# Three scatters in flight with a GpSimd memset between them, and k2's seven products in another order

## The chip, the cores and the metric

The kernel runs on one core of one Trainium2 chip. The metric is the device time of one launch, in microseconds (us). Runs that are shown as "time" are launches without a profile; the profiled execution is one more launch, recorded by the hardware profiler, and its time is given beside them.

## The reference

One graph-attention layer and one gated feed-forward block over 384 nodes with 1024 features, both with a residual. Cut to what matters:

```
xn   = layernorm(x)                                   # 384 x 1024
q,k,v    = xn@wq.T+bq, xn@wk.T+bk, xn@wv.T+bv
q2,k2,v2 = q@wiq.T+biq, k@wik.T+bik, v@wiv.T+biv       # 16 heads of 64
mask = full((384,384), -inf); mask[src,dst] = softplus(w)[type-1]   # 12288 edges,
                                                      # the last edge of a cell wins
mask[i,i] = softplus(w)[3] where it is still -inf
out  = softmax(q2 k2^T / 8 + mask) v2                 # per head
x    = x + out@wo.T + bo
h    = silu(xn2@w1.T*s1) * (xn2@w2.T*s2)              # xn2 = layernorm(x)
h    = gelu(h@h1.T*..); h = gelu(h@h2.T*..)
x    = x + h@w3.T*s3
```

Edges are sorted by dst. Edge e lies in column e // 128 and partition e % 128 of a 128 x 96 table, so there are 96 mask columns of 128 edges each.

## The kernel before, in words

**Stages.** Layer normalisation and transposes come first, then the projections q, q2, v, v2, k and k2, then attention in 24 units (8 pairs of heads times 3 row tiles), the output projection, and the feed-forward block. The order on SyncE, ScalarE, VectorE and TensorE is the order of the program text (`manual_schedule`); on GpSimd only what is wrapped in `keep_in_program_order` is held to it.

**The mask.** The mask is built in a table in HBM, `tab`, with one word for each of the 147456 cells and some spare cells behind them. First a transfer fills it with the values without edges. Then each of the 96 columns is written by one indirect DMA on GpSimd (L366, the *scatter*), which puts 128 words of `val` at the cells of `cell`. Two scatters that are in flight together must not write the same cell. So VectorE first compares every edge of column c with the later edges of the columns that can be in flight with it (L350, `targets`), and an edge that has a later twin there is sent to a spare cell. `DEEP = 3` columns are in flight at most. The function `flight` says how many there are at column c: three in the groups of 16 columns that are listed in `DENSE`, and two in group 3 (columns 48 to 63). A scatter waits for the landing of the one that is `flight(c)` before it. Columns are handled in chunks of eight (`chunk`: `targets`, then `scatter`, then the next load of keys), and the calls of `chunk` are spread over the projections q to v2. When all 96 have been issued, GpSimd waits for the last three to land, reads the table back into SBUF as `mask` (L575) and goes on to its weight loads (L101: two halves of wo, later the feed-forward weights).

**Memory of the mask stage.** The tiles of this stage (`jp`, `bare`, `key`, `cell`, `val` and others in the pool `edge`, the key rows in the pool `krow`) are given back before attention; the pool `attn` is laid over the same addresses and holds, among others, `s1`, `s2`, `s4` of k2, the exponentials `e` and the transposed probabilities `pTb`.

**Products with seven multiplications.** The projections q2, v, v2, k and k2 use a 2 x 2 block scheme with seven block products instead of eight. It needs sums of blocks of the input (a11, a12, a21, a22; the sums are s1 to s4) and of the weights (b11, b12, b21, b22), which are formed in place: b12 becomes b22-b12 ahead of the products, b11 becomes b11+b12, b12 becomes b22-b11, b21 becomes b21-b11. For k2 these are in `project_k2` (L633): each entry of its list is a weight block, an input block and the work that VectorE or ScalarE does on the product, and a product lies in one of two PSUM buffers (`ps_mm`, `bufs=2`). The first half of k2 runs in one piece (L746) after its sums of the input have begun at L744; the second half is issued in small shares between the attention slots (L770).

What the sums of the input depend on and where they stand before:

```
nc.vector.tensor_add(s1, a21, a22)                       # L744
minus(s2, s1, a11)                                       # L745, shown as L414
for step, _ in enumerate(project_k2(0, slice(0, 2), 0)): # L746
    if step == 2 * HK:
        minus(a21, a11, a21)                             # a21 becomes s3, in place
        minus(s4, a12, s2)
```

Of the kernel before, what the change touches and what calls it, by code (L numbers as in the profile page):

```python
# [9 lines left out]
FP = mybir.dt.float32  # L10
# [14 lines left out]
P = 128  # L25
# [3 lines left out]
NCOL = E // P  # L29
HN = N // 2  # L30
HK = KF // 2
DEEP = 3
DENSE = (0, 1, 2, 4, 5)
CHUNK = 8
CELLS = N * N
EPS = 1e-5
# [8 lines left out]
def gnn_ffn_kernel(ctx: ExitStack, tc: tile.TileContext, x, edges, etw, vecs, rows,  # L45
# [4 lines left out]
    nc = tc.nc  # L50
# [148 lines left out]
    with tc.tile_pool(name="edge", bufs=1) as ep, tc.tile_pool(name="krow", bufs=2) as krp, \  # L199
# [114 lines left out]
        cnt = ep.tile([P, NCOL], FP, name="cnt")  # L314
        cell = ep.tile([P, NCOL], I32, name="cell")
        val = ep.tile([P, NCOL], FP, name="val")

        def values():

            ty = ep.tile([P, NCOL], I32, name="ty")  # L320
            nc.vector.tensor_scalar(ty, ed[:, 2, :], 3.0, None, op0=ALU.add)
            ty3 = ep.tile([P, NCOL], I32, name="ty3")
            nc.vector.tensor_single_scalar(ty3, ty, 3, op=ALU.bitwise_and)
            for j in range(4):
                vj = ep.tile([P, NCOL], FP, tag="vj", name="vj")
                nc.vector.tensor_scalar(vj if j else val, ty3, float(j), w8[:, j:j + 1],
                                        op0=ALU.is_equal, op1=ALU.mult)
                if j:
                    nc.vector.tensor_add(val, val, vj)
# [7 lines left out]
                                                    ap=[[0, P], [P, n], [1, P]]))  # L337
            return kr.rearrange("p c j -> p (c j)")

        def flight(c):  # L340

            return DEEP if c // 16 in DENSE else DEEP - 1

        def targets(c0, krf):

            for j in range(CHUNK):
                c = c0 + j
                w = min(flight(c + DEEP - 1), NCOL - c) * P
                jk = krp.tile([P, DEEP * P], BF, tag="jk", name="jk")
                nc.vector.scalar_tensor_tensor(jk[:, :w], krf[:, j * P:j * P + w], key[:, c:c + 1],  # L350
                                               later[:, :w], op0=ALU.is_equal, op1=ALU.mult,
                                               accum_out=cnt[:, c:c + 1])
            s = slice(c0, c0 + CHUNK)
            lost = krp.tile([P, CHUNK], FP, tag="lost", name="lost")
            nc.vector.scalar_tensor_tensor(lost, cnt[:, s], 0.0, spare, op0=ALU.is_gt, op1=ALU.mult)
            nc.vector.tensor_tensor(cell[:, s], key[:, s], lost, op=ALU.max)

        sent = []

        def after(ins, earlier):  # L360
            tc.add_manual_dep(ins, earlier.name, mybir.DependencyInfo(
                mybir.DependencyClass.Sync, mybir.DependencyReason.DATA), reason="table")

        def scatter(c0):
            for c in range(c0, c0 + CHUNK):
                i = nc.gpsimd.indirect_dma_start(  # L366
                    out=tab, in_=val[:, c:c + 1], in_offset=None,
                    out_offset=bass.IndirectOffsetOnAxis(ap=cell[:, c:c + 1], axis=0)).ins
                for other in sent[max(c - flight(c) + 1, 0):]:
                    tc.declare_no_dep(i, other, reason="no cell in common")  # L370
                for other in sent[max(c - DEEP, 0):max(c - flight(c) + 1, 0)]:
                    after(i, other)
                sent.append(i)

        krs = []
        asked = iter(range(0, NCOL, CHUNK))
# [7 lines left out]
        def chunk(more=True):  # L384

            c0 = len(sent)
            targets(c0, krs.pop(0))
            if c0 == 0:
                values()
            scatter(c0)  # L390
            if more:
                ask()
# [20 lines left out]
        def minus(to, a, b):  # L413
            nc.vector.tensor_tensor(to, a, b, op=ALU.subtract)  # L414

        def quarters(src, n):

            return [src[:, k:k + HK, r:r + n] for r in (0, n) for k in (0, HK)]

        def row_sums(src, n, **place):  # L420

            sums = act.tile([P, 4, HK, n], FP, name="sums", **place)
            s1, s2, s3, s4 = (sums[:, i] for i in range(4))
            a11, a12, a21, a22 = quarters(src, n)
            minus(s3, a11, a21)
            nc.vector.tensor_add(s1, a21, a22)
            minus(s2, s1, a11)
            minus(s4, a12, s2)
            return s1, s2, s3, s4
# [12 lines left out]
        def paired(w, g):  # L442

            w = w.rearrange("p k (g h c) -> p k g h c", h=2, c=P)[:, :, g]
            return [w[:, k:k + HK, :, h] for k in (0, HK) for h in (0, 1)]

        def paired_third(w):
            b11, b12, b21, b22 = paired(w, slice(0, 2))
            minus(b12, b22, b12)
# [59 lines left out]
        with tc.tile_pool(name="ps_st", bufs=6, space=bass.MemoryType.PSUM) as ps_st:  # L509
# [23 lines left out]
            c11, c12, c21, c22 = (v2[:, t, c:c + FH] for t in (0, 1) for c in (0, FH))  # L533
# [7 lines left out]
            def block(x, w):  # L541
                return product_R([(x[:, k, :], w[:, k, :]) for k in range(HK)])
# [8 lines left out]
            s1, s2, s3, s4 = row_sums(vT, P, tag="t", bufs=2)  # L551
# [6 lines left out]
            m7 = block(s3, b12)  # L558
            minus(b12, b22, b11)
            m6 = block(s2, b11)  # L560
            m2 = block(a12, b21)
# [4 lines left out]
            m5 = block(s1, b12)  # L566
# [49 lines left out]
    with tc.tile_pool(name="attn", bufs=1) as ap, \  # L616
# [7 lines left out]
        s1, s2, s4 = (ap.tile([P, HK, HN], FP, name=f"s{i}") for i in (1, 2, 4))  # L624
        a11, a12, a21, a22 = quarters(kT, HN)
# [3 lines left out]
        def flush():  # L629
            while waiting:  # L630
                waiting.pop()()

        def project_k2(half, g, lag):  # L633


            b11, b12, b21, b22 = paired(wik[half], g)
            c = k2T[:, 4 * half:4 * half + 4, :].rearrange("p (g h) n -> p g h n", h=2)[:, g]
            c11, c12, c21, c22 = (c[:, :, h, r:r + HN] for r in (0, HN) for h in (0, 1))
            n = g.stop - g.start

            def copies(ps):
                nc.scalar.copy(c11, ps)
                nc.scalar.copy(c12, ps)
                nc.vector.tensor_add(b11, b11, b12)

            def finish(to, ps, more, h):
                for i in range(n):
                    o = BIK + 4 * half + 2 * (g.start + i) + h
                    nc.vector.scalar_tensor_tensor(to[:, i, :], ps[:, i, :], vec[:, o:o + 1],  # L649
                                                   more[:, i, :], op0=ALU.add, op1=ALU.add)  # L650

            def m2(ps):
                finish(c11, ps, c11, 0)
                minus(b21, b21, b11)

            def m7(ps):
                nc.vector.tensor_add(c22, ps, c12)
                minus(b12, b22, b11)

            def m5(ps):  # L660
                nc.vector.tensor_add(c12, ps, c12)
                finish(c22, ps, c22, 1)

            for w, x, use in ((b11, a11, copies), (b21, a12, m2),
                              (b11, s2, lambda ps: nc.vector.tensor_add(c12, ps, c12)),
                              (b12, a21, m7), (b21, a22, lambda ps: finish(c21, ps, c22, 0)),
                              (b12, s1, m5), (b22, s4, lambda ps: finish(c12, ps, c12, 1))):
                ps = ps_mm.tile([P, 2, 256], FP, tag="mm", name="ps")
                for i in range(n):
                    for k in range(HK):  # L670
                        nc.tensor.matmul(ps[:, i, :HN], lhsT=w[:, k, i, :], rhs=x[:, k, :],  # L671
                                         start=(i, k) == (0, 0), stop=(i, k) == (n - 1, HK - 1))
                        if i * HK + k == lag - 1:
                            flush()
                        yield
                waiting.append(lambda ps=ps[:, :n, :HN], use=use: use(ps))
                if lag == 0:
                    flush()
            if g.stop == 2:
                early.append(load_w(*ffn[half], rounded=True))  # L680
# [61 lines left out]
        loaded = small.tile([P, 1], FP, name="loaded")  # L742
        nc.scalar.activation(loaded, eps, AF.Exp)
        nc.vector.tensor_add(s1, a21, a22)  # L744
        minus(s2, s1, a11)  # L745
        for step, _ in enumerate(project_k2(0, slice(0, 2), 0)):  # L746
            if step == 2 * HK:
                minus(a21, a11, a21)
                minus(s4, a12, s2)
        paired_third(wik[1])  # L750
        k2 = chain(*(project_k2(1, slice(g, g + 1), 3) for g in range(2)))
        steps, done, pairs = 2 * 7 * HK, 0, 0
        for s, new in enumerate(slots):
# [8 lines left out]
            for i in range(2):  # L762
# [6 lines left out]
                if i == 0:  # L769
# [7 lines left out]
                    if s in (9, 10):  # L777

                        ps = ps_mm.tile([P, 512], FP, tag="mm", name="ps")
# [226 lines left out]
```

## Time and profile before

| what | value |
|---|---|
| time, median of 3 runs | 404.39 us (403.07 to 406.37) |
| profiled execution, its own time | 408.77 us |
| its span, first to last instruction | 406.7 us |
| TensorE busy | 385.8 us, 95% of the span |
| VectorE busy | 258.7 us, 64% |
| GpSimd busy | 126.4 us, of which 116.2 us are the 96 scatters |
| mean granted TensorE clock | 0.983 |

The span is shorter than the profiled execution's own time by 2.1 us, which lie around it. The profiled execution is 4.4 us longer than the median of the runs; a sum of durations from the profile is made against 408.77 us. In the profile a line of the timeline reads: start, duration, engine, source line, operation, output and inputs, count, and in brackets how long the engine sat idle before it and what ended that.

### The profile page before, as it was taken

The page shows a single profiled execution, that of the slowest core. Times are in us where ns is not written, and L with a number is a line of the kernel's source. Part 1 is how long each engine was busy: PE and PEld are TensorE (multiplying, and loading weights), DVE is VectorE, ACT ScalarE, POOL GpSimd, SP SyncE. Part 2 cuts the span into 40 slices and gives each one's busy share as a digit, 9 for nine tenths or more (in the row PEclk, how much of TensorE's full clock was granted, in tenths as well). Part 3 has the DMA queues.
Part 4 walks back from the last instruction along what each step waited for, and adds up shares of the span by engine and source line. Part 5 has one row for each costly group of instructions (what it writes and reads, how often), then busy time and mean ns, then how long its engine had stood idle before and what let it go on. Part 6 is the DMA issues. An engine that isn't in the chain of part 4 may idle for free.

```text
span 406.7 us, 5195 instructions
## 1 busy us (share of the span) xinstructions
PE 385.8 (95%) x1925; PEld 294.0 (72%) x1925; DVE 258.7 (64%) x664; ACT 103.4 (25%) x233; POOL 126.4 (31%) x116
## 2 busy tenths in 40 slices
PE   7899999999999999999689988899999999999993
PEld 7555589999997444899479955566555444699983
DVE  5695959985898777454237587878766115622455
ACT  4611110000000000200000056775555138332420
POOL 3033447786764488568730000000000000200000
PEclk9999999999999999999959999999999999999998
DMA  7799996357227500940057072220941400290004
GB/s 275 260 356 277 302 327 236 93 191 262 66 66 264 201 0 2 358 158 2 0 187 285 0 233 80 63 93 6 318 144 53 156 0 0 67 348 0 1 4 155
DMA packets 29227, 59.90 MB, mean 147 GB/s; under 512 B 5424, under 2 KB 8336, under 8 KB 29072
## 3 DMA queue, kind: packets, MB, share of 16 engines
q1 hardware_dynamic: 20976, 45.90, 32.9%
q0 software_dynamic: 7936, 13.23, 10.6%
q10 hardware_dynamic: 288, 0.41, 0.3%
q8 instruction: 17, 0.28, 0.3%
q14 instruction: 10, 0.08, 0.1%
HBM read 57.26 MB, written 2.26 MB: 146 GB/s over the span
## 4 chain that ended last, share of the span: by engine, by line
PE 86%; DVE 8%; ACT 2%; issue 2%; DMA 1%; SPq 0%; ACTq 0%
PE ps L457 28%; PE ps L601 10%; PE ps L151 10%; PE ps L538 9%; PE ps L671 7%; PE ps L870 6%; PE av L730 4%; PE ps L882 4%; PE pp L721 3%; PE sc L689 3%; DVE e L703 2%; DVE e L713 1%; DMA xs<-in_x 1%; DVE y L965 1%; DVE y L964 1%
## 5 line engine op out<-in xcount | busy, mean ns | idle before, releaser
L366 POOL DMA_INDIRECT tab<-val,cell x96 | 116.2, 1210 | 84.3 <-DMA tab<-val,cell 32.2
L350 DVE SCALAR_TENSOR_TENSOR jk<-kr,key,jp 128x384 bf16<-128x384 f32 (+1 forms) x96 | 50.3, 588 | 5.7 <-DMA kr<-keyd 5.7
L601 PE MATMUL ps<-wo,aT 128*128 128x512 f32 x96 | 43.0, 595 | 0.0
L151 PE MATMUL ps<-xT,wq 128*128 128x384 f32 x128 | 41.5, 487 | 0.3 <-ACT xT L266 0.3
L151 PEld LDWEIGHTS ps<-xT,wq 128*128 128x128 f32 x128 | 24.2, 190 | 17.2 <-ACT xT L266 0.5
L705 ACT ACTIVATE e<-e,lo 128x384 f32<-128x384 f32 x48 | 29.0, 605 | 27.5 <-DVE lo L703 27.4
L601 PEld LDWEIGHTS ps<-wo,aT 128*128 128x128 f32 x96 | 17.5, 190 | 19.4 <-issue 18.5
L870 PE MATMUL ps<-x,w 128*128 128x384 f32 (+2 forms) x176 | 25.8, 306 | 0.0
L457 PE MATMUL ps<-xT,wk 128*128 128x192 f32 x96 | 21.2, 374 | 4.7 <-issue 4.6
L101 POOL DMA_DIRECT2D w<-in_w x3 | 2.5, 847 | 74.1 <-PE ps L671 54.5
L870 PEld LDWEIGHTS ps<-x,w 128*128 128x128 f32 x176 | 25.1, 190 | 0.5 <-issue 0.5
L703 DVE CUSTOM_DVE_ANT_0 e<-sc,mask 128x384 f32<-128x384 f32 x48 | 23.9, 553 | 1.0 <-PE sc L689 1.0
L538 PE MATMUL ps<-wiv,vT 128*128 128x512 f32 x56 | 24.5, 592 | 0.0
L457 PEld LDWEIGHTS ps<-xT,wk 128*128 128x128 f32 x96 | 19.0, 222 | 7.1 <-issue 7.0
L721 PEld LDWEIGHTS pp<-ident,e 128*128 128x128 f32 x144 | 16.2, 141 | 10.9 <-issue 6.7
L671 PE MATMUL ps<-kT,wik 128*128 128x192 f32 x128 | 22.8, 328 | 1.1 <-DVE k2T L649 1.1
L671 PEld LDWEIGHTS ps<-kT,wik 128*128 128x128 f32 x128 | 20.7, 190 | 2.2 <-DVE k2T L649 2.0
L457 PE MATMUL ps<-sums,wk 128*128 128x192 f32 x128 | 21.5, 327 | 0.5 <-issue 0.5
L457 PEld LDWEIGHTS ps<-sums,wk 128*128 128x128 f32 x128 | 20.9, 190 | 0.9 <-issue 0.7
L721 PE MATMUL pp<-ident,e 128*128 128x128 f32 x144 | 20.6, 278 | 0.7 <-ACT pTb L766 0.5
L457 PE MATMUL ps<-sums,wiq 128*128 128x192 f32 x128 | 21.1, 326 | 0.0
L457 PE MATMUL ps<-sums,wv 128*128 128x192 f32 x128 | 21.1, 326 | 0.0
(168 smaller groups left out, 591.7 us busy)
## 6 DMA issues: line engine op xcount, KB each, us to landing
kr<-keyd SPq DMA_DIRECT2D x11, 640.0 KB
raw<-in_w SPq DMA_DIRECT2D x12, 512.0 KB
w<-in_w POOLq DMA_DIRECT2D x3, 2048.0 KB
wiq<-in_wiq SPq DMA_DIRECT2D x2, 2048.0 KB
wv<-in_wv SPq DMA_DIRECT2D x2, 2048.0 KB
wiv<-in_wiv SPq DMA_DIRECT2D x2, 2048.0 KB
wk<-in_wk SPq DMA_DIRECT2D x2, 2048.0 KB
wik<-in_wik SPq DMA_DIRECT2D x2, 2048.0 KB
```

The lines of the kernel that those rows point to most:

```text
L151: nc.tensor.matmul(ps[:, :N], lhsT=w[:, k, o * P:(o + 1) * P], rhs=src[:, k, :], start=(k == 0), stop=(k == nk - 1))
L350: nc.vector.scalar_tensor_tensor(jk[:, :w], krf[:, j * P:j * P + w], key[:, c:c + 1], later[:, :w], op0=ALU.is_equal, op1=ALU.mult, accum_ ...
L366: i = nc.gpsimd.indirect_dma_start(out=tab, in_=val[:, c:c + 1], in_offset=None, out_offset=bass.IndirectOffsetOnAxis(ap=cell[:, c:c + 1], ...
L457: nc.tensor.matmul(ps[o // 2][:, o % 2, :HN], lhsT=w[:, k, o * P:(o + 1) * P], rhs=x[:, k, :], start=(o % 2, k) == (0, 0), stop=(o % 2, k) ...
L538: nc.tensor.matmul(ps, lhsT=x, rhs=w, start=i == 0, stop=i == len(steps) - 1)
L601: nc.tensor.matmul(ps, lhsT=aT[:, k, t * P:(t + 1) * P], rhs=wos[half][:, k, :], start=k == start, stop=k == end - 1)
L671: nc.tensor.matmul(ps[:, i, :HN], lhsT=w[:, k, i, :], rhs=x[:, k, :], start=(i, k) == (0, 0), stop=(i, k) == (n - 1, HK - 1))
L703: nc.vector.tensor_tensor_reduce(e, sc[:, :N], mask[:, t, :], -0.125, 3e38, op0=ALU.add, op1=ALU.min, accum_out=lo)
L705: nc.scalar.activation(e, e, AF.Exp, bias=lo, scale=-1.0, accum_out=dens[u][:, j:j + 1])
L721: nc.tensor.transpose(pt[:, m, :], e[:, m * P:(m + 1) * P], ident)
L730: nc.tensor.matmul(av[j * D:(j + 1) * D, :N], lhsT=v2[:, m, h * D:(h + 1) * D], rhs=pTs[pair % 2][:, j * NT + m, :], start=(m == 0), stop= ...
L870: nc.tensor.matmul(ps[:, rows], lhsT=w[:, k, o * P:(o + 1) * P], rhs=x[:, k, rows], start=n == 0, stop=n == len(todo) - 1)
```

## The change

1. `DENSE` and `flight` go. Every column may have three scatters in flight, and every `targets` instruction compares over three columns (384 numbers wide, where 16 of them were 256 wide).
2. After each scatter GpSimd writes zeros into a new tile `pace` of 128 x 512 float32. Scatter and memset are both kept in program order, so that one memset lies between any two scatters, and one behind the last.
3. `project_k2` takes its seven products in another order. Product by product, as weight block times input block, before: b11 a11, b21 a12, b11' s2, b12 s3, b21' a22, b12' s1, b22 s4. After: b11 a11, b21 a12, b12 s3, b22 s4, b11' s2, b21' a22, b12' s1. A prime marks a weight block that has been replaced in place by a sum. The product b11' s2 is now added to two outputs (c12 and c22) by two instructions where one sufficed.
4. All four sums of the input (s1, a21 replaced by s3, s2, s4) are formed before the first product of k2's first half; two of them were formed during its second product.

```
-DENSE = (0, 1, 2, 4, 5)
+PACE = 512
...
+        pace = ep.tile([P, PACE], FP, name="pace")
...
-                w = min(flight(c + DEEP - 1), NCOL - c) * P
+                w = min(DEEP, NCOL - c) * P
...
-                i = nc.gpsimd.indirect_dma_start(
+                send = nc.gpsimd.indirect_dma_start(
                     out=tab, in_=val[:, c:c + 1], in_offset=None,
-                    out_offset=bass.IndirectOffsetOnAxis(ap=cell[:, c:c + 1], axis=0)).ins
-                for other in sent[max(c - flight(c) + 1, 0):]:
+                    out_offset=bass.IndirectOffsetOnAxis(ap=cell[:, c:c + 1], axis=0))
+                tc.keep_in_program_order(send)
+                i = send.ins
+                for other in sent[1 - DEEP:]:
                     tc.declare_no_dep(i, other, reason="no cell in common")
-                for other in sent[max(c - DEEP, 0):max(c - flight(c) + 1, 0)]:
-                    after(i, other)
+                if c >= DEEP:
+                    after(i, sent[-DEEP])
                 sent.append(i)
+                tc.keep_in_program_order(nc.gpsimd.memset(pace, 0.0))
...
+            def m6(ps):
+                nc.vector.tensor_add(c12, ps, c12)
+                nc.vector.tensor_add(c22, ps, c22)
...
-            for w, x, use in ((b11, a11, copies), (b21, a12, m2),
-                              (b11, s2, lambda ps: nc.vector.tensor_add(c12, ps, c12)),
-                              (b12, a21, m7), (b21, a22, lambda ps: finish(c21, ps, c22, 0)),
-                              (b12, s1, m5), (b22, s4, lambda ps: finish(c12, ps, c12, 1))):
+            for w, x, use in ((b11, a11, copies), (b21, a12, m2), (b12, a21, m7),
+                              (b22, s4, lambda ps: finish(c12, ps, c12, 1)), (b11, s2, m6),
+                              (b21, a22, lambda ps: finish(c21, ps, c22, 0)), (b12, s1, m5)):
...
         nc.vector.tensor_add(s1, a21, a22)
+        minus(a21, a11, a21)
         minus(s2, s1, a11)
-        for step, _ in enumerate(project_k2(0, slice(0, 2), 0)):
-            if step == 2 * HK:
-                minus(a21, a11, a21)
-                minus(s4, a12, s2)
+        minus(s4, a12, s2)
+        for _ in project_k2(0, slice(0, 2), 0):
+            pass
```

## The prediction

> **What bounds the kernel now.** I read the page first, then the waits of GpSimd, then the timeline around the place where mask and k2 meet, the table by stage for the clock, and last the waits of TensorE in the attention part.
>
> ```profile
> PE 385.8 (95%) x1925; PEld 294.0 (72%) x1925; DVE 258.7 (64%) x664; ACT 103.4 (25%) x233; POOL 126.4 (31%) x116
> PE 86%; DVE 8%; ACT 2%; issue 2%; DMA 1%; SPq 0%; ACTq 0%
> L366 POOL DMA_INDIRECT tab<-val,cell x96 | 116.2, 1210 | 84.3 <-DMA tab<-val,cell 32.2
> ```
>
> TensorE holds 86% of the chain that ended last, GpSimd none of it. But 96 scatters of 1.21 us, each with a gap of 0.30 us ahead of it, fill the time from 26.4 to 204.6 us, and this stream has little to spare:
>
> ```profile
> POOL tab L366 <- DMA tab<-val,cell: 32.2, 15, 4.7
> POOL tab L366 <- issue: 23.3, 75, 0.8
> POOL tab L366 <- DVE jk L350: 3.8, 3, 2.1
> ```
>
> Only some 38 us are real waiting, 32.2 us of it for landings. The rest is work and the gap. Where the stream ends:
>
> ```profile
> 188.85 2.28 DVE L414 TENSOR_TENSOR wk<-wk 128x2048 f32<-128x2048 f32 x1
> 189.72 2.25 POOL L366 DMA_INDIRECT tab<-val,cell  x1 [0.30 <-issue]
> 192.27 0.96 POOL L366 DMA_INDIRECT tab<-val,cell  x1 [0.31 <-issue]
> ...
> 202.39 0.96 POOL L366 DMA_INDIRECT tab<-val,cell  x1 [0.30 <-issue]
> 203.65 0.96 POOL L366 DMA_INDIRECT tab<-val,cell  x1 [0.30 <-issue]
> ...
> 206.42 0.80 POOL L575 DMA_DIRECT2D mask<-tab  x1 [1.81 <-DMA tab<-val,cell]
> ...
> 213.13 0.96 DVE L744 TENSOR_TENSOR s<-kT 128x768 f32<-128x768 f32 x1
> ...
> 230.45 0.92 PE L689 MATMUL sc<-k2T,q2T 64*128 64x384 f32 x4
> ...
> 232.35 0.55 DVE L703 CUSTOM_DVE_ANT_0 e<-sc,mask 128x384 f32<-128x384 f32 x1
> ```
>
> See three things. The last scatters run back to back, 1.265 us apart. The last one lands just ahead of 206.4 us, when the read of the mask starts. And L744, the first sum of k2's input, starts at 213.13 us. L744 writes into the memory that the mask stage gave back. The views leave semaphore instructions out, but the records of the trace hold four of them at L744, from 212.4 to 212.7 us, which name the eight counters on which the scatters land. So k2's sums wait for the last of the 96 scatters, not only for kT. Before, the scatters are 7 us early (206.4 against 213.1 us).
>
> The 7 us are a loan: kT itself is late, because TensorE stumbles while the last scatters run.
>
> ```profile
> 190.00:196.00 6.00, 6.00 (x38) 5.88 (x37) 1.69 (x2) 0.00 (x0) 4.85 (x4) 1.00 0.02 0
> 200.00:202.00 2.00, 0.78 (x4) 0.50 (x3) 0.00 (x0) 0.00 (x0) 1.70 (x2) 0.92 0.02 1
> 202.00:204.00 2.00, 0.99 (x4) 0.77 (x4) 0.00 (x0) 0.00 (x0) 1.39 (x3) 0.50 0.02 0
> 208.00:212.00 4.00, 4.00 (x15) 4.00 (x14) 0.84 (x3) 0.00 (x0) 0.17 (x1) 0.51 0.95 319
> ```
>
> (Columns: stretch, length, busy us and count of PE, PEld, DVE, ACT, POOL, then clock, DMA share, GB/s.) From 196.4 to 206.8 us only 16 matmuls run, where 16 x 0.163 us = 2.6 us would do; the next 17 take 5.5 instead of 2.8 us at half clock. That is 10.5 us lost, and it ends with the last landing. No wait is named; the scatters are the only other thing going on.
>
> **What the Trainium skill says.** *Perfetto Trace Analysis*, section "DMA Instruction — SWDGE (GPSIMD)": the recorded end of such a DMA is that of its descriptors, not of its data. The trace agrees: the last scatter ends at 204.6 us and its landing is still waited for until 206.4. *SBUF — State Buffer*, "Who interferes with whom": a VectorE instruction with two SBUF inputs holds up a GpSimd instruction that reads SBUF, not one that only writes. The trace agrees on the first half: the scatter at 189.72 us lasts 2.25 us, until the L414 of 188.85 us ends. A memset only writes. *TensorE: Matmul & The Clock Gate*, "What's actually happening": idleness of a few us halves the clock until it has been busy for a while. Here it stayed at 0.50 from about 202 to 212 us.
>
> **The change part by part.**
>
> *The memset.* Nearest rows, from the start of the profile:
>
> ```profile
> 0.74 0.20 POOL masks.py:197 MEMSET ident<- 128x128 f32 x1 [0.29 <-POOLq L998]
> 0.89 1.06 POOL L209 MEMSET mask<- 128x1152 f32 x1
> ```
>
> (1.06-0.20)/1024 = 0.84 ns per number, so 512 numbers last 0.20 + 384 x 0.00084 = 0.52 us. Starts of neighbours overlap by 0.05 us (0.74+0.20 against 0.89), which leaves 0.48 us of the queue for each, 46 us in all. Bounds: if the 0.30 us gap ahead of a scatter passes while the memset runs, only about 0.20 us each are added; if the memset pays such a gap of its own, 0.78. I take 0.48: when a scatter had waited for a landing it also began 0.27 us after it, so the gap looks like work of GpSimd itself, which a memset on the same engine can't hide; and the small memsets at the start follow each other within 0.03 us, so a memset has no such gap.
>
> *Where the scatters then end.* Columns 0 to 19 (26 to 72 us) are bound by landings, with 16 us of waits: memsets fall mostly into them. I give this stage 3 us more, 75 us. Then no wait is left to speak of, since three periods of 2 us cover the 2 to 6 us of a landing, and the two-in-flight waits of columns 51, 53 and 55 (7.8 us in all) go. The period is the scatter's mean in its stretch + 0.30 + 0.48. Means by stretch: 72 to 113 us 30.88/24 = 1.29; 113 to 143 16.26/14 = 1.16; 143 to 178 25.04/19 = 1.32; 178 to 206 20.73/20 = 1.04. So 24 columns at 2.07 reach 125 us; 9 at 1.94 reach 143; 17 at 2.10 reach 178; 13 at 1.82 reach 202; the last 12 at 0.96 + 0.78 = 1.74, with VectorE standing, start until 223, and the last lands 2 us later: **225 us** instead of 206.
>
> *What waits for it.* L744 on VectorE, and behind it in order the other sums, all of b11', b21', b12' and the evictions that free PSUM. TensorE can do products 1 and 2 (5.2 us) and stops at product 3, which needs s3. The mask read, wo and the feed-forward weights queue behind the scatters on GpSimd too, but mask was there some 20 us before L703 asked for it, and is again early: it is read at 225 us and asked for at about 245. L744 moves from 213.1 to 225.1 us: +12.0. Whether TensorE's stumble goes doesn't matter then; what it saves is waited away.
>
> *From L744 to L703.* Before 232.35 - 213.13 = 19.2 us. After: s1 and s3 take 2.0 us (0.96 + 0.95 and the hand-over); products 3 to 7 are 5 x 16 x 0.163 = 13.0, the first of them at half clock after the idle stretch, +2.6; then add 0.56, finish 0.74, L414 1.22: 20.1. So +0.9. The other two sums, b11' and b21' (0.95 + 0.95 + 1.22 + 0.74 + 1.22 us) fit beside products 3 and 4.
>
> *k2's second half.* Its stops of TensorE in the attention part:
>
> ```profile
> PE ps L671 <- DVE wik L644: 1.9, 1, 1.9
> PE ps L671 <- DVE wik L414: 1.7, 1, 1.7
> ```
>
> b11' and b12' now have two and one more products of slack, so these 3.6 us can go; against them stand two extra adds of 0.35 us on VectorE, which is the next in the chain there. Bounds -3.6 to +0.7; I take -2.
>
> *The rest.* 16 `targets` instructions are 128 numbers wider: about 0.13 us each on VectorE, which has 27 us free between 72 and 143 us. Nothing.
>
> Sum: +12.0 + 0.9 - 2 = +10.9 on 408.8, 419.7 us in the profile's own time. That time was 4.4 us over the median of the runs; the same offset gives **415 us** for the median.
>
> **The rivals.**
>
> *A, the stumble goes and the stream is in time (faster).* If the gap of 0.30 us passes under the memset, 76 columns gain 0.27 each: the end is about 225 - 20 = 205, landing 206. TensorE, no longer disturbed by back-to-back scatters, reaches k2 at 202 and product 3 at 207 instead of 217; L744 at 206 lets it start at 208. That is -9.5 and -2, with no cold clock: 397 us in the profile's time, 393 on the median; if the runs without a profile stumble less (they are 4.4 us shorter), about 400. I put it at 397. It decides once the scatters land before 210. For it: the stumble ends with the last landing. Against: the 0.27 us after a landing.
>
> *B, a draw.* Scatters land at 211 to 215: what the stumble gave is taken by the wait. About 404 us. It needs a memset of 0.3 us.
>
> *C, worse.* The memset pays its own gap partly: 0.64 each, landing at 237, +24 instead of +12: 427 us.
>
> *D, the memset does not space the scatters* (GpSimd works on both at once): then 7.8 us of waits go, landing near 198, the stumble stays and kT with it; -2 from the second half: 402 us.
>
> **How the numbers follow.** Forecast (landing 217 to 232) 0.58; C 0.09; A 0.19; B 0.09; D 0.05. The forecast's own range is 408 to 422 us. The 80% range takes C's edge and most of A: 396 to 427. A measurement of this kernel can tell about 1% from no change. Faster by over 1% (below 400.3): 0.21; within 1%: 0.12; slower (above 408.4): 0.67.
>
> **What would show it.** Right: starts of scatters 1.7 us apart where nothing else disturbs, L744 beginning within a us of the last landing, a hole in TensorE of over 8 us after k2's second product, half clock behind it; no stop at L644 or L414 later. Wrong: scatters still 1.3 us apart, or L744 later than the last landing by several us. The forecast falls if the last scatter starts before 210 us.

## The result, and the profile after

The changed kernel takes 423.19 us (median of 4 runs, 420.57 to 423.53) against 404.62 us before (median of 4 runs, one more than in the table of before): a ratio of 1.0443, 95% interval 1.0384 to 1.0503. It is slower by 4.4%. The profiled execution after took 423.14 us with a span of 421.3 us; against the profiled span before, 406.7 us, that is +14.6 us.

The page of the changed kernel, the lines that answer to those shown of before (busy time and share by engine; the chain; then line, engine, operation, count, busy us, mean ns, idle time before):

```profile
PE 383.2 (91%) x1925; PEld 293.7 (70%) x1925; DVE 261.4 (62%) x667; ACT 103.4 (25%) x233; POOL 180.8 (43%) x212
PE 47%; POOL 27%; DVE 9%; DMA 9%; issue 4%; ACT 2%; SPq 0%; POOLq 0%; ACTq 0%; DVEq 0%
L363 POOL DMA_INDIRECT tab<-val,cell x96 | 118.9, 1238 | 52.3 <-DVE val L330 22.0
L373 POOL MEMSET pace<- 128x512 f32 x96 | 51.9, 541 | 0.1
```

TensorE does the same work (383.2 us busy), but its part of the chain has fallen from 86% to 47%, and GpSimd, which held none of it, holds 27%: the scatters (L363) and the memsets (L373) have become the path that sets the end. The 51.9 us of memsets are new; what the scatters waited for landings fell from 32.2 to 16.6 us, as GpSimd's waits show (who waited for what: us in total, times, longest):

```profile
POOL tab L363 <- DMA tab<-val,cell: 16.6, 15, 2.8
POOL mask L575 <- DMA tab<-val,cell: 1.3, 1, 1.3
```

The timeline of the changed kernel where mask and k2 meet:

```profile
223.97 0.97 POOL L363 DMA_INDIRECT tab<-val,cell  x1 [0.17 <-issue]
224.94 0.54 POOL L373 MEMSET pace<- 128x512 f32 x1
225.64 0.96 POOL L363 DMA_INDIRECT tab<-val,cell  x1 [0.17 <-issue]
...
227.90 0.96 DVE L747 TENSOR_TENSOR s<-kT 128x768 f32<-128x768 f32 x1 [25.70 <-DMA tab<-val,cell]
228.40 0.79 POOL L575 DMA_DIRECT2D mask<-tab  x1 [1.26 <-DMA tab<-val,cell]
...
229.99 4.24 PE L674 MATMUL ps<-kT,wik 128*128 128x192 f32 x16 [23.38 <-DVE kT L414]
...
246.92 0.55 DVE L706 CUSTOM_DVE_ANT_0 e<-sc,mask 128x384 f32<-128x384 f32 x1
```

Read the brackets. The first sum of k2's input (L747, which was L744) stood still for 25.70 us, and a landing in `tab` released it. TensorE had done products 1 and 2 by 206.6 us and then waited 23.38 us for the block that replaces a21. The table by stage shows the hole and the half clock behind it (stretch, length, busy us and count of PE, PEld, DVE, ACT, POOL, clock, DMA share, GB/s):

```profile
206.00:212.00 6.00, 0.62 (x4) 0.32 (x2) 0.00 (x0) 0.00 (x0) 5.50 (x8) 0.75 0.01 0
212.00:220.00 8.00, 0.00 (x0) 0.00 (x0) 0.00 (x0) 0.00 (x0) 7.17 (x11) 0.50 0.01 0
230.00:238.00 8.00, 8.00 (x41) 8.00 (x42) 6.94 (x10) 0.00 (x0) 1.02 (x2) 0.82 1.00 356
```

From 212 to 220 us GpSimd is the only one of these engines that works. Before the hole, from 196 to 206 us, TensorE no longer stumbles: its last product of kT ends at 201.4 us in place of 212.3. Those 11 us are waited away.

### The profile page after: what moved, and what is told of

The parts are those of the page before. It is cut to its first block, busy times and chain, and to the rows that moved or that the text cites. A ratio compares the mean times of both kernels' runs of the same rounds, so it can differ in the third digit from the quotient of the medians.

```text
span 421.3 us, 5295 instructions
## 1 busy us (share of the span) xinstructions
PE 383.2 (91%) x1925; PEld 293.7 (70%) x1925; DVE 261.4 (62%) x667; ACT 103.4 (25%) x233; POOL 180.8 (43%) x212
## 4 chain that ended last, share of the span: by engine, by line
PE 47%; POOL 27%; DVE 9%; DMA 9%; issue 4%; ACT 2%; SPq 0%; POOLq 0%; ACTq 0%; DVEq 0%
POOL tab L363 19%; PE ps L601 10%; PE ps L151 10%; POOL pace L373 8%; DMA tab<-val,cell 8%; PE ps L873 6%; PE ps L674 6%; PE av L733 4%; PE ps L885 4%; PE pp L724 3%; PE sc L692 2%; DVE e L706 2%; PE ps L457 1%; DVE e L716 1%; DMA xs<-in_x 1%
## 5 line engine op out<-in xcount | busy, mean ns | idle before, releaser
L363 POOL DMA_INDIRECT tab<-val,cell x96 | 118.9, 1238 | 52.3 <-DVE val L330 22.0
L347 DVE SCALAR_TENSOR_TENSOR jk<-kr,key,jp 128x384 bf16<-128x384 f32 (+1 forms) x96 | 52.5, 611 | 4.4 <-DMA kr<-keyd 4.4
L373 POOL MEMSET pace<- 128x512 f32 x96 | 51.9, 541 | 0.1
L674 PE MATMUL ps<-kT,wik 128*128 128x192 f32 x128 | 25.6, 349 | 27.7 <-DVE kT L414 23.4
L674 PEld LDWEIGHTS ps<-kT,wik 128*128 128x128 f32 x128 | 22.4, 203 | 29.4 <-issue 23.6
L101 POOL DMA_DIRECT2D h<-in_h x2 | 1.5, 752 | 62.7 <-issue 62.7
L457 PEld LDWEIGHTS ps<-sums,wiq 128*128 128x128 f32 x128 | 20.9, 190 | 0.0
```

Of the source, the lines that this page charges most:

```text
L363: send = nc.gpsimd.indirect_dma_start(out=tab, in_=val[:, c:c + 1], in_offset=None, out_offset=bass.IndirectOffsetOnAxis(ap=cell[:, c:c + ...
L373: tc.keep_in_program_order(nc.gpsimd.memset(pace, 0.0))
L457: nc.tensor.matmul(ps[o // 2][:, o % 2, :HN], lhsT=w[:, k, o * P:(o + 1) * P], rhs=x[:, k, :], start=(o % 2, k) == (0, 0), stop=(o % 2, k) ...
```

## The experiments

The theory under test: the scatters' last landing gates k2's first sum, because attention's memory was the mask stage's, and the memset moves this landing. Rivals: the new order of k2's products costs the time; or the hole has another cause. Each kernel of this section was timed beside runs of the kernel before on its own chip; ratios are against those. "Landing" is the time at which the read of the mask starts. The read waits for the last landing and starts about 0.6 us behind it (in the changed kernel the last scatter started at 225.64 us and landed 2.13 us later, at 227.77), so a first sum that the landing releases stands some 0.5 us before the figure in this column. The times to the right of the ratio are those of one profiled execution each. In three of these (k2's order only, reused memory out of the way, before without its last 20 scatters) TensorE had also stood still for 1.6, 2.1 and 2.5 us near 77 us: VectorE, late after a late load of keys, was late with an eviction of q2. What follows there comes 2 to 3 us later for that reason alone.

| kernel | time, us | ratio, 95% interval | landing, us | k2's first sum, us | first exponential, us |
|---|---|---|---|---|---|
| before (profile shown above) | 404.62 | 1 | 206.4 | 213.1 | 232.3 |
| changed | 423.19 | 1.0443 (1.0384 to 1.0503) | 228.4 | 227.9 | 246.9 |
| no memset | 398.93 | 0.9871 (0.9792 to 0.9951) | 204.4 | 203.9 | 222.5 |
| k2's order only | 401.64 | 0.9935 (0.9906 to 0.9965) | 210.1 | 209.6 | 228.7 |
| scatter part only | 424.28 | 1.0497 (1.0411 to 1.0583) | 227.2 | 226.7 | 247.1 |
| changed, reused memory out of the way | 410.55 | 1.0153 (1.0072 to 1.0234) | 228.9 | 204.8 | 233.4 |
| memset of 64 | 401.57 | 0.9912 (0.9869 to 0.9954) | 208.5 | 208.0 | 226.6 |
| memset of 1024 | 452.9 (one run) | | 257.8 | 257.2 | 277.8 |
| no memset, memory out of the way | 399.81 | 0.9877 (0.9833 to 0.9921) | 206.0 | 207.0 | 225.7 |
| before, once more | 402.84 (one run) | | 206.7 | 207.5 | 225.9 |
| memory out of the way, tail paced | 398.20 | 0.9827 (0.9778 to 0.9877) | 214.0 | 202.5 | 222.2 |
| no memset, memory out of the way, again | 400.53 | 0.9880 (0.9824 to 0.9935) | 206.0 | 207.0 | 225.6 |
| before, without its last 20 scatters | 398.12 | 0.9823 (0.9775 to 0.9871) | 181.8 | 205.3 | 224.5 |

**One part away: no memset.**

```
-                tc.keep_in_program_order(nc.gpsimd.memset(pace, 0.0))
```

> The changed kernel without the memset: three scatters in flight throughout, k2's new order. Theory (the landing of the last scatter gates k2's first sum): scatters 1.27 us apart again, the two-in-flight waits gone, so the last landing is at 196 to 200 us in place of 227.7; the first sum starts when kT is done, 201 to 212 us, and the time is 394 to 404 us. Rival (the new order of the products costs the time): it stays at 418 to 424 us. Rival (the stumble of TensorE comes from back-to-back scatters): PE has a hole ahead of the last landing again, near 190 to 199 us, and half clock.

Measured: 398.93 us. The loss is gone and a gain is left. Three in flight and the fixed order on GpSimd are still in this kernel, so neither of them carries the loss. The last landing came at about 204 us, some 4 us later than expected, since 18 waits for landings still took 30.9 us: without the memset, three in flight fill up again. The group of k2's first sum in this kernel, its idle time last:

```profile
L745 DVE TENSOR_TENSOR s<-kT 128x768 f32<-128x768 f32 x1 | 1.0, 959 | 1.6 <-DMA tab<-val,cell 1.6
```

Even here the landing releases the sum, 1.6 us after kT would have. The stumble that one rival expected was not there in this profile; TensorE's longest gap between 180 and 223 us was 0.2 us.

**One part alone: k2's order.** `DENSE`, `flight` and `scatter` as before, k2's list and sums as changed.

> The kernel before with only k2's new order of products and the sums ahead of it. Theory (the scatters carry the loss): within 1% of before, 401 to 408 us; the attention part from the first exponential to the end is as long as in the changed kernel (174.4 us). Rival (the order costs): 415 us or more.

Measured: 401.64 us, 0.65% below before. The order is no cost. From the first exponential to the end of the span it is 402.3 - 228.7 = 173.6 us, against 174.4 before: within a us of no effect. The profile shows one thing more. The scatters of before are all in this kernel, TensorE did not stumble, and so the landing itself held up the first sum:

```profile
L747 DVE TENSOR_TENSOR s<-kT 128x768 f32<-128x768 f32 x1 | 1.0, 957 | 5.4 <-DMA tab<-val,cell 5.4
```

So the wait for the scatters lay close to deciding in the kernel before already.

**The other part alone: the scatters.** The new scatter code with k2's old list and sums.

> The changed kernel with k2's old order of products and sums: only the memset and three in flight are left of the change. Theory: the last landing again near 227 us, the first sum right behind it, 421 to 426 us. Rival (the order costs): 403 to 410 us.

Measured: 424.28 us. The whole loss is in this part. The first sum of its k2:

```profile
L744 DVE TENSOR_TENSOR s<-kT 128x768 f32<-128x768 f32 x1 | 1.0, 958 | 24.0 <-DMA tab<-val,cell 24.0
```

From this sum to the first exponential it is 247.1 - 226.7 = 20.4 us with the old order and 19.0 with the new, both after a hole: by these two profiles the new order is worth 1.4 us in the first half.

**The wait alone taken away.** The scatters stay as slow; what they and the memset touch lies elsewhere.

```
-        cell = ep.tile([P, NCOL], I32, name="cell")
-        val = ep.tile([P, NCOL], FP, name="val")
-        pace = ep.tile([P, PACE], FP, name="pace")
+        cell = const.tile([P, NCOL], I32, name="cell")
+        val = const.tile([P, NCOL], FP, name="val")
+        pace = const.tile([P, PACE], BF, name="pace")
```

> The changed kernel with the tiles that scatters and memset touch (cell, val, pace) kept out of the memory that attention takes over; pace is bfloat16 with as many numbers. The scatters stay as slow. Theory: k2's first sum no longer waits and starts near 202 us, k2's first half is done at about 220 us, and now the first exponential waits for the read of the mask, which can't begin before 228 us: first exponential at 232 to 235 us in place of 246.9, 408 to 412 us. Rival (the hole in TensorE has another cause than the reused memory): first exponential stays at about 247 us, 421 to 424 us.

Measured: 410.55 us. This shows the mechanism. The landing is where it was, and k2's first sum starts at 204.8 us all the same (here: count, shortest, middle and longest duration in ns, first and last start):

```profile
L747 DVE TENSOR_TENSOR s<-kT x1: 1011/1011/1011, 204.8 to 204.8; 128x768 f32<-128x768 f32 x1
L575 POOL DMA_DIRECT2D mask<-tab x1: 794/794/794, 228.9 to 228.9; - x1
```

That takes 12.6 of the 18.6 us of loss away. Of the three tiles `cell` and `val` are enough for the wait: the kernel without the memset has no `pace`, and its first sum waited too. The next thing in line is the one expected, the read of the mask, for which the first exponential now waits:

```profile
L706 DVE CUSTOM_DVE_ANT_0 e<-sc,mask 128x384 f32<-128x384 f32 x48 | 24.0, 552 | 10.2 <-DMA mask<-tab 8.8 <-PE sc L692 1.4
```

**The suspected cost, an eighth and double.** `PACE = 64` and `PACE = 1024`.

> The changed kernel with a memset of 64 numbers in place of 512. Theory (the period of the scatters sets the end): by the 0.84 ns per number a memset lasts 0.54 - 448 x 0.00084 = 0.16 us; with a gap of 0.17 us the period is 0.965 + 0.165 + 0.17 = 1.30 us, hardly above the 1.265 us without a memset, so the last landing is at 203 to 208 us and the time 398 to 403 us. Rival (any instruction between two scatters costs a fixed 0.3 us or more): last landing near 225 us, 418 us or more.

> The changed kernel with a memset of 1024 numbers: the suspected cost doubled. Theory: 512 x 0.00084 = 0.43 us more for each of the 76 columns that do not wait for landings, some for the first 20: last landing near 260 to 266 us in place of 227.7, k2's first sum right behind it, time 455 to 463 us. Rival (the stream is slowed by landings or VectorE, not by the memset itself): below 440 us.

Measured: 401.57 and 452.9 us. Where nothing disturbs, the starts of two scatters lie 1.265 us apart without a memset, 1.29 us with 64 numbers, 1.67 with 512 and 2.10 with 1024: 0.84 ns for each number, (2.10-1.29)/960. With 64 the landing is at 208.5 us, half a us later than expected, and the kernel is a little faster than before: a memset adds no fixed 0.3 us. With 1024 the landing was at 258 us, a little under the 260 expected, and the time of its single run just under its range. The time follows the landing one to one: from 512 to 1024 numbers the first sum moves by 257.2 - 227.9 = 29.3 us, the span by 451.0 - 421.3 = 29.7.

**Without memset and without the gate.** The first experiment with `cell` and `val` moved to `const`.

> No memset, three in flight, k2's new order, and cell and val kept out of the memory that attention takes over. Theory: k2's first sum starts when kT is done (about 202 us) and no longer waits 1.6 us for the scatters; the read of the mask begins near 204 us and is long done at the first exponential, so nothing of the mask stage is left on the chain: 395 to 398 us, 1.6 to 2.5% below before. Rival (the reused memory matters only where the scatters are slow): as without the memset alone, 398 to 400 us.

Measured: 399.81 us, not better than without the memset alone; the expected 395 to 398 us were missed, and the rival's range was met. The first sum no longer waits for scatters, but it started at 207.0 us, not 202: TensorE stumbled again, with gaps of 0.4 to 0.5 us between 202 and 206 us, and VectorE began the last evictions of kT at 205.6 us, though TensorE had been done with kT at 202.2:

```profile
202.67 1.05 PE L672 MATMUL ps<-kT,wik 128*128 128x192 f32 x4 [0.51 <-issue]
...
205.53 6.76 PE L672 MATMUL ps<-kT,wik 128*128 128x192 f32 x40 [0.51 <-issue]
205.61 1.39 DVE L475 SCALAR_TENSOR_TENSOR kT<-ps,vec,kT 128x192 f32<-128x192 f32 x4 [3.58 <-remote]
```

**Before, once more.**

> The kernel before once more, for its profile. Asked: does TensorE stumble again at 196 to 207 us while the last scatters run 1.27 us apart? If back-to-back scatters cause it: again a loss of about 10 us with half clock. If it belongs to single executions: no gap over 0.4 us there, kT done near 201 us, and k2's first sum waits for the last landing near 206 us, with a time of 401 to 405 us.

Measured: 402.84 us, and the answer lies in between. TensorE was done with kT at 201.6 us and then stumbled in k2's first two products, for a shorter time than in the first profile and at full clock:

```profile
203.74 1.05 PE L671 MATMUL ps<-kT,wik 128*128 128x192 f32 x4 [0.51 <-issue]
205.18 0.74 PE L671 MATMUL ps<-kT,wik 128*128 128x192 f32 x3 [0.40 <-issue]
205.90 1.60 DVE L477 SCALAR_TENSOR_TENSOR kT<-ps,vec,kT 128x192 f32<-128x192 f32 x4 [5.66 <-remote]
```

Again it ended with the last landing (the mask read starts at 206.74 us). So the stumble comes back, but its size differs from execution to execution: 10.5 us lost in the first profile, about 3 here (products 1 and 2 took 8.1 us, where the changed kernel's took 5.4). Nor did the first sum wait for the landing here: VectorE evicted the last of kT only from 205.90 to 207.50 us, and the sum followed at once, at 207.53.

**What makes TensorE stumble.** Three kernels: a memset behind the last 20 scatters only, beside the same kernel without any memset; and the kernel before without its last 20 scatters.

```
-                tc.keep_in_program_order(nc.gpsimd.memset(pace, 0.0))
+                if c >= 76:
+                    tc.keep_in_program_order(nc.gpsimd.memset(pace, 0.0))
...
-            for c in range(c0, c0 + CHUNK):              # the kernel before
+            for c in range(c0, min(c0 + CHUNK, 76)):
```

> As the kernel with cell and val kept out of the reused memory, but with the memset of 512 numbers behind the last 20 scatters only (columns 76 to 95). Theory (back-to-back scatters make TensorE stumble, spaced ones do not): the last landing moves to about 212 us, the mask read is still in time for the first exponential near 220 us, TensorE has no gap over 0.35 us between 195 and 220 us, and the time is 396 to 398 us, with less spread than without any memset. Rival (the stumble has another cause): gaps as without a memset, 398 to 402 us. Rival (the mask read becomes late): first exponential waits for it, 400 us or more.

> The kernel with no memset and the reused memory out of the way, once more beside the one with a paced tail. If the stumble comes with back-to-back scatters: gaps in TensorE in the last ten us before the last landing in this profile or a spread of 2 us and more over the runs; median 398 to 400.5 us, 1 to 3 us above the paced tail. If not: both kernels the same.

> The kernel before without its last 20 scatters (columns 76 to 95 are never written to the table; all else as before). If these scatters cause the stumble, and if they gate k2: last landing near 180 us, no gap in TensorE at 195 to 210 us in any execution, k2's first sum at 202 to 203 us, 397 to 399 us with a spread under 2 us. If the stumble belongs to that point of the program, whatever GpSimd does: gaps there again, times spread over 398 to 405 us.

Measured: 398.20, 400.53 and 398.12 us. The paced tail (runs from 397.41 to 399.12) is 2.3 us shorter than its twin without a memset (398.81 to 402.46), 0.6%; it came out 0.2 us above its expected range, and its landing at 214.0 us, not 212. From the first experiment, without the memset alone (ratio 0.9871, timed on another chip), it can't be told apart. Its stages, where the unpaced ones stumble:

```profile
202.00:206.00 4.00, 4.00 (x27) 4.00 (x26) 3.90 (x6) 0.86 (x2) 3.56 (x5) 1.00 0.03 4
206.00:212.00 6.00, 6.00 (x39) 6.00 (x38) 4.99 (x7) 0.00 (x0) 5.45 (x7) 1.00 0.01 0
```

TensorE is busy throughout at full clock. Without the memset there were gaps of up to 0.93 us again at 204 to 205 us. With the last 20 scatters left out there is no gap in that place. There two expectations were missed: the first sum came at 205.3 us, not 202 to 203, and the runs spread over 3.2 us, not 2. The profiled execution, at 400.83 us, is the one far run; the 2.5 us near 77 us that it lost are named above. The other six lie within 0.8 us.

Counted over all profiles: of the six kernels or executions with back-to-back scatters at the end, four stumbled (before twice, and the one without memset and gate twice) and two didn't (no memset; k2's order only); of the seven with a memset there or no scatters, none did. If the scatters had nothing to do with it, four stumbles strewn over thirteen profiles would all fall among these six about once in 48 times. So the counts, and the twin of the paced tail, speak for the scatters; they are no proof. It is open whether the pause or the memset helps: with 64 numbers the starts lie 1.29 us apart, hardly more than 1.265, and its one profile has no stumble either. By what path scatters reach TensorE is open too. The data that they move can hardly be it: the DMA share in the stumbling stretches is 0.01 to 0.02.

## Why the prediction was right, and where it was off

- **The gate.** Right: L747 waits for the last of the 96 scatters, and with the reused memory out of the way it doesn't. That before had 7 us to spare only because kT was late fits too: in the second profile of before, with a smaller stumble, the first sum came 0.8 us after the read of the mask began, and with k2's order alone and no stumble it waited 5.4 us for the landing.
- **The memset.** Taken at 0.48 us of the queue; 0.41 measured (1.67 against 1.265), although the instruction itself is 0.54 us long and not 0.52. That a memset isn't held up by VectorE came out: six of them ran wholly inside an L414 and took 0.54 to 0.55 us, while scatters took up to 3.08. One reading was a little off: the scatter of 189.72 us did not end with the L414 (191.13 us) but 0.84 us after it, at 191.97. The argument that the 0.30 us gap ahead of a scatter is GpSimd's own work and can't be hidden was half wrong: it shrank to 0.17.
- **Where the scatters end.** First sum at 225.1 predicted, 227.9 measured. Column 20 started at 75.2 us (75 predicted) and column 44 at 124.7 (125). "No wait is left to speak of" was a miss: in the stretches with weight loads landings took up to 7.4 us, more than the 5.0 us of three periods, and from column 20 on 4.8 us of waiting over the gap were left. The scatters themselves also lasted 3.9 us longer in sum than priced. Against these 8.7 us stand 5.4 us that the memset and the gap together cost less than priced. So the landing came out within 3 us partly by luck: two errors of opposite sign. One mean was also read too low: the 14 scatters that start between 113 and 143 us took 17.39 us, 1.24 each and not 1.16, because the last of them runs past 143. It did no harm, as the nine columns priced with it took 1.15 each.
- **From the first sum to the first exponential.** 20.1 predicted, 19.0 measured. The clock came back sooner: the first product after the hole lasted 4.1 us (229.99 to 234.07), not 5.2.
- **k2's second half.** -2 predicted, 0 measured: 174.4 us from the first exponential to the end, before and after. TensorE's stops at L644 and L414 went, as said. Others took their place, which its waits in the attention part of the changed kernel show:

```profile
PE ps L674 <- DVE k2T L649: 3.3, 2, 1.9
PE ps L674 <- ACT k2T L643: 1.1, 1, 1.1
```

They release TensorE by evicting a product, and a product may start only when one of the two PSUM buffers is free; before, such a wait stood at L649 once, with 1.1 us. With the weight sums out of the way the buffers are what is late next.

- **The median.** The sum in the profile's own time was 419.7 us, 3.4 below the 423.14 measured: +2.8 for the landing, -1.1 and +2 for the two stretches, the small rest outside the span. The median of 423.19 us lies above the forecast's own range of 408 to 422, though the landing lies within its 217 to 232; the 80% range holds it. The step that failed is the last one, "the same offset gives 415". The 4.4 us between the profile and the median of before were most likely stumble. No trace of a median execution was kept, but of the 23 executions of before that were timed beside the first experiments the shortest took 401.0 us at a mean granted clock of 0.996 and the longest 408.94 at 0.983, the clock of the profiled one. The prediction itself says that whatever the stumble costs is waited away in the changed kernel, so there was nothing to subtract: after the change the profiled execution and the median agree within 0.1 us. Without that step the forecast is 420.
- **The rivals.** The one on the other side needed landings before 210 us. Where runs made that so (no memset, a memset of 64), the kernel was faster than before, at 399 to 402 us; so its deciding point was well placed, but a memset of 512 didn't reach it. The costlier memset (0.64 us each) and the memset that doesn't space the scatters did not come: it was 0.41 us each, with starts 1.67 us apart.

## What to carry to other kernels

Before slowing an engine that is "off the path", look for what its end releases, also through memory that a later stage takes over: such a wait shows no idle time as long as something else ends later. Put a delay only where it is wanted: the same memset on the last 20 columns, with the gate out of the way, gives 0.9827 (0.9778 to 0.9877) of the time where on all 96 with the gate it gave 1.0443; against its twin without a memset that is 2.3 us, so most of the gain comes from what else was changed. And when a profiled execution is longer than the median, ask which stretch is the odd one before carrying the difference over to a kernel in which that stretch is covered.

## What the runs showed of the hardware

- While scatters ran back to back on GpSimd (starts 1.265 us apart, 128 words each), TensorE stumbled in four of six profiles: gaps of mostly 0.4 to 1.1 us between groups of one to four matmuls that wait for nothing named. In the first profile of before three matmuls came every 2.12 us, in the second three or four every 1.4 us. VectorE was late as well: in the second profile it began to evict kT 4.3 us after TensorE was done with it (201.56 to 205.90 us). Each time it ended with the last landing, within 0.6 us of the start of the mask read. With starts 1.67 us apart it was in none of four profiles.
- A GpSimd memset of 128 x 512 float32 costs its queue 0.41 us between two scatters: it lasts 0.54 us and takes 0.13 us off the gap ahead of the next scatter (0.30 to 0.17). Beyond that it is 0.84 ns for each number. With bfloat16 it lasts as long (0.54 us).
- A scatter of 128 words lands 2.13 us after its start while the DMA engines are nearly idle (columns 77 to 95 of the changed kernel, 2.12 to 2.16 us, DMA share 0.01 to 0.02). While they are nearly full (share 0.90 from 26 to 75 us), columns 0 to 14 took 5.4 to 8.5 us.
